# Attention and quantized convolution block: start, first block and seams reordered, with filler products on TensorE

## The chip, the core and the metric

The kernel runs on one core of a Trainium2 chip. The metric is the device time of one execution in microseconds (us); the median of three runs of the kernel before is 2590.27 us (2589.32 to 2590.64). The engines are TensorE (PE: products, with its weight loads PEld), VectorE (DVE), ScalarE (ACT), GpSimd (POOL) and SyncE (SP, which here only issues DMAs). Each works through its own queue in order and waits for the others by semaphores. Products are written to PSUM, which DVE and ACT read.

## What is computed

x has 4 images of 128 channels by 64 x 64 positions, all in float32. First attention with 4 heads of 32 channels over 4096 positions of an image, then a residual block of two 3x3 convolutions with quantized weights:

```python
x_norm = _group_norm(x, norm_w, norm_b)              # 8 groups of 16 channels
qkv = jnp.einsum('oc,bchw->bohw', qkv_w, x_norm) + qkv_b[None, :, None, None]
...
attn = jax.nn.softmax(jnp.einsum('bhid,bhjd->bhij', q, k) * scale, axis=-1)
out = jnp.einsum('bhij,bhjd->bhid', attn, v)
...
x = x + jnp.einsum('oc,bchw->bohw', proj_w, out) + proj_b[None, :, None, None]
...
out = conv3x3_decomposed(x, lsq_quantize(w1, alpha1))
out = jax.nn.relu(batchnorm(out, gamma1, beta1))     # mean and variance over all 4 images
out = conv3x3_decomposed(out, lsq_quantize(w2, alpha2))
out = jax.nn.relu(batchnorm(out, gamma2, beta2) + x)
```

Each batch norm needs the statistics of the whole convolution before its first output can be made. So there is a seam between the convolutions, and another before the final ReLU, at which the last statistics have to come through.

## The kernel before

**Stages.** Lines 564 to 585: image 0 is loaded in 8 chunks of 512 columns (tiles xh0 and xh1, four chunks each), its group statistics are made, and the first chunks of k, q and v. Lines 589 to 710: attention, in 32 blocks of 512 queries (4 images by 8), each with 32 steps kt of 128 keys. Lines 714 to 796: first convolution. Lines 798 to 837: second convolution. Lines 838 to 846: final sum, ReLU and store.

**A step of attention.** `scores` makes a half step: 4 products s (line 425, q and k each split into a high and a low part), and an exponential on ACT (427) into a tile p. `weights` adds p times v to acc (438), and p to a running sum on DVE (450); six of the 32 steps (MOVED) add theirs by a DMA of POOL instead (443, 445). PE's order is written out by hand: 3 half steps of scores, 1 step of weights, 3 half steps, 2 steps. Scores run ahead of weights. One such cycle of three steps has some 6.2 us of PE work, and more where side work is due.

**Side work.** `schedule` lists functions with the step kt after which they are emitted. In block n = 0 (lines 624 to 630) these are the remaining chunks of k, q and v of image 0: 16 or 32 products in two halves (301) into a bank of PSUM, then, one step later, the evacuation: for k and q the high part on ACT (335) and the low part on DVE (336), for v one addition on DVE (355). k and q go by a store on POOL's queue (340) to DRAM, and come back in another layout by SP's loads (394 for k, 405 for q). `load_q` of the next block is emitted at step 14. The first chunks, k_0 and q_0, go straight from the staging tile to their place (`direct`, lines 375 to 387), with 8 DMAs each, over SP and POOL in turns.

**PSUM and buffers.** Pool pss has 3 tiles of two banks (scores, the first chunks, later the convolution tiles), pool psa 2 tiles of one bank: acc holds one of them all through a block, and all side products take turns with the other. ppool has 8 tiles, for p and, at the start, for xh0, xh1 and the staging of the first chunks; a tile comes free when its last reader is done.

**Group statistics.** `norm_parts` returns steps that run alternately on DVE and PE: zero (aggregate the statistics of the chunks), one (average the means over a group by a product with gavg, gm), two (variance of the group's parts, dv), three (product gv), four (reciprocal root with POOL's power, scale ga, offset gc, scaled weights wn), five (products gb of the offsets with the weights, for the biases of k and q, and of v), six (add the biases). For image 0 they run in one go; for images 1 to 3 they are side work two blocks ahead.

**Convolutions.** The image is cut into 16 bands of 16 rows (4 images by 4); a band has two halves of 512 columns. `conv` makes 18 products for a half (9 taps by a high and a low part of the input, 722). `layer` runs the bands: both halves into one tile of two banks, `prepare` (splits or ReLUs of a coming band), then for each half statistics on DVE (774) and a copy to SBUF on ACT (775). At the end `batch_norm` aggregates the statistics of all 32 halves and makes scale and offset; in the second layer's input they are applied by `relu_rows`: ReLU on ACT into t (802), a rounding copy to hi (805) and the difference lo (806) on DVE.

Of the kernel before, what the change touches and what calls it, by code (L numbers as in the profile page):

```python
# [16 lines left out]
F32 = mybir.dt.float32  # L17
# [61 lines left out]
def _fast_body(ctx, tc, x, norm_w, norm_b, qkv_wt, qkv_b, proj_wt, proj_b,  # L79
# [31 lines left out]
    warm = const.tile([P, 1], F32, name="warm")  # L111
    nc.scalar.activation(warm, mhalf, AF.Exp)
# [124 lines left out]
    def norm_parts(b, st):  # L237
# [13 lines left out]
        def two():  # L251
            nc.vector.tensor_copy(mean, gm[0][:, 0:1])
            nc.vector.tensor_tensor(dv, mv[:, 0:1], mean, ALU.subtract)
            nc.vector.tensor_tensor(dv, dv, dv, ALU.mult)
            nc.vector.tensor_tensor(dv, dv, mv[:, 1:2], ALU.add)
# [5 lines left out]
        def four():  # L261
# [4 lines left out]
            nc.vector.tensor_tensor(c, mean, a, ALU.mult)  # L266
            nc.vector.tensor_tensor(c, nb, c, ALU.subtract)
# [7 lines left out]
        def five():  # L275
# [4 lines left out]
            nc.tensor.matmul(gm[2][:, P : 2 * P], cb, wqkv[:, 2 * P : 3 * P], start=True, stop=True)  # L280

        def six():
            b2 = wpool.tile([P, 2], F32, name=f"b2_{b}", tag="b2")
            nc.vector.tensor_tensor(b2, gm[2][:, 0:2], bkq, ALU.add)
            bvn = wpool.tile([P, P], F32, name=f"bvn{b}", tag="bvn")
            nc.vector.tensor_tensor(bvn, gm[2][:, P : 2 * P], bv, ALU.add)
            norm[b] = norm[b][0], b2, bvn

        return zero, one, two, three, four, five, six
# [4 lines left out]
    qs, ks, vs = {}, {}, {}  # L294

# [7 lines left out]
    def project_parts(b, j, xin, start=False):  # L303
# [5 lines left out]
        def bank(what):  # L309
            if start:  # L310
# [64 lines left out]
    def direct(what, t):  # L375

        u = k_tile(0, 0) if what == "k" else q_tile(0, 0)
        for g in range(2):
            for s in range(4):
# [3 lines left out]
                eng = (nc.sync, nc.gpsimd)[s % 2]  # L383
# [68 lines left out]
    def finish_parts(n):  # L452
# [30 lines left out]
        def sums_at_once():  # L483
# [6 lines left out]
            weigh()  # L490
            most = [small.tile([P, 1], F32, name=f"most{i}") for i in range(2)]
# [35 lines left out]
        return dict(copy=copy, merge=merge, sums=sums, sums_at_once=sums_at_once, spread=spread, invert=invert, gather=gather,  # L527
# [37 lines left out]
    for j in range(NB):  # L565
        eng = (nc.sync, nc.scalar)[j % 2]
        eng.dma_start(out=halves[j // 4][:, j % 4, :], in_=x_chunk(0, j))
    st = small.tile([P, NB, 6], F32, name="st0", tag="st")
    for j in range(NB):
        nc.vector.bn_stats(st[:, j, :], halves[j // 4][:, j % 4, :])  # L570
    for f in norm_parts(0, st):
        f()
# [8 lines left out]
    for what, j in (("k", 0), ("q", 0), ("k", 1), ("v", 0), ("k", 2), ("v", 1), ("k", 3), ("v", 2)):  # L581
        for f in first_chunk(j, what, True):
            f()
        if what == "v":
# [9 lines left out]
    def schedule(n, before):  # L594
# [27 lines left out]
        if n + 1 < len(blocks):  # L622
            add(14, lambda: load_q(*blocks[n + 1]))
# [682 lines left out]
```

## Time and profile before

The profiled execution took 2589.98 us; its span from the first to the last instruction is 2588.2 us. All times below are in us from the start of that span.

| what | where | time |
|---|---|---|
| x chunk 0, then chunk 1 reach DVE | start | 3.82, 8.48 |
| statistics of image 0 done | 570 | 13.02 |
| first products of k (pk) begin | 301 | 18.68 |
| first score product | 425 | 29.05 |
| first exponential, first acc product | 427, 438 | 30.45, 34.39 |
| last acc product of block 0 ends | 438 | 114.8 |
| first convolution product | 722 | 2265.87 |
| last product of the first layer ends | 722 | 2408.71 |
| first product of the second layer | 722 | 2415.49 |
| last product of the second layer ends | 722 | 2555.25 |
| first store of the output issued | 846 | 2562.62 |
| last store issued, end of the span | 846 | 2580.6, 2588.2 |

A busy share is an average over all these stages. What an edit is worth is read where it works: which engine waits there, for what, and whether something later waits for that engine.

### The profile page before, as it was taken

To read this page: it belongs to the slowest core of one execution; us is meant where nothing else is said; L and a number is where in the kernel's file an instruction comes from. 1 tells how busy PE (TensorE), PEld (TensorE's weight loads), DVE (VectorE), ACT (ScalarE), POOL (GpSimd) and SP (SyncE) were. 2 spreads that over 40 slices of the span, in tenths; PEclk is the share of its full clock that TensorE was granted. 3 is DMA by queue.
4 is the path that set the end of the run, shared out by engine and by line. 5 is a ranking of instruction groups with operands and counts; after the bars stand their busy time and mean duration, and the time that the engine had idled before them with its cause. 6 is when DMAs were issued, how large, how long until landed. Compare 5 with 4: busy or idle time off the path is not lost.

```text
span 2588.2 us, 48399 instructions
## 1 busy us (share of the span) xinstructions
PE 2517.2 (97%) x20394; PEld 1223.4 (47%) x20394; DVE 2140.3 (83%) x1402; ACT 2081.9 (80%) x2275; POOL 281.4 (11%) x456
## 2 busy tenths in 40 slices
PE   6999999999999999999999999999999999999894
PEld 3444444444444444444444444444444444477773
DVE  5898888888988898888988988888999998953344
ACT  4888899999988999999988899999889898911223
POOL 2111111111011111110011111110000000100000
PEclk9999999999999999999999999999999999999997
DMA  5876766698667767697667666986655757634004
GB/s 160 191 187 172 177 161 149 154 206 201 162 148 178 178 155 171 149 225 171 160 171 161 164 159 150 207 202 142 151 130 126 154 126 148 146 80 145 1 1 164
DMA packets 147417, 400.04 MB, mean 155 GB/s; under 512 B 59240, under 2 KB 60008, under 8 KB 118648
## 3 DMA queue, kind: packets, MB, share of 16 engines
q0 software_dynamic: 45888, 280.59, 47.9%
q1 hardware_dynamic: 100728, 115.23, 16.8%
q8 instruction: 162, 2.65, 0.4%
q10 hardware_dynamic: 576, 1.05, 0.1%
q14 instruction: 63, 0.52, 0.1%
HBM read 105.32 MB, written 55.83 MB: 62 GB/s over the span
## 4 chain that ended last, share of the span: by engine, by line
PE 88%; DVE 5%; issue 3%; DMA 2%; ACT 1%; POOL 0%; SPq 0%; DVEq 0%; POOLq 0%; ACTq 0%
PE s L425 39%; PE acc L438 34%; PE c L722 9%; DVE r L450 3%; DMA rm<-p 2%; PE l L467 1%; PE po L301 1%; PE pk L301 1%; PE pq L301 1%; PE pv L301 1%; ACT p L427 1%; DVE res L844 1%; DMA xh<-in_x_dram 0%; DMA q<-qst 0%; DVE st L570 0%
## 5 line engine op out<-in xcount | busy, mean ns | idle before, releaser
L427 ACT ACTIVATE p<-s 128x1024 f32<-128x1024 f32 x2048 | 1940.2, 1034 | 235.0 <-PE s L425 158.7
L450 DVE TENSOR_TENSOR r<-r,p 128x2048 f32<-128x2048 f32 x768 | 1758.4, 2290 | 97.3 <-ACT p L427 48.1
L425 PE MATMUL s<-q,k 64*128 64x512 f32 x8192 | 1162.3, 413 | 3.9 <-ACT p L427 2.2
L438 PE MATMUL acc<-p,v 128*32 128x512 f32 x8192 | 1021.1, 601 | 0.6 <-DVE v L355 0.6
L425 PEld LDWEIGHTS s<-q,k 64*128 64x128 f32 x8192 | 711.7, 185 | 631.9 <-issue 298.0
L438 PEld LDWEIGHTS acc<-p,v 128*32 128x32 f32 x8192 | 198.6, 109 | 453.7 <-issue 446.3
L445 POOL DMA_DIRECT2D rm<-p x160 | 138.6, 866 | 950.7 <-ACT p L427 783.6
L775 ACT COPY cv<-c 128x512 f32<-128x512 f32 x64 | 37.6, 587 | 220.8 <-DVE st L774 220.8
L722 PE MATMUL c<-hi,wq 128*128 128x512 f32 x576 | 150.1, 405 | 8.3 <-DVE hi L805 6.8
L722 PE MATMUL c<-lo,wq 128*128 128x512 f32 x576 | 148.1, 402 | 0.0
L774 DVE BATCH_NORM_STATS2 st<-c 128x6 f32<-128x512 f32 x64 | 44.7, 699 | 124.5 <-PE c L722 102.5
L722 PEld LDWEIGHTS c<-hi,wq 128*128 128x128 f32 x576 | 109.4, 191 | 40.1 <-issue 8.9
L722 PEld LDWEIGHTS c<-lo,wq 128*128 128x128 f32 x576 | 109.0, 189 | 28.9
L448 DVE TENSOR_TENSOR r<-p,p 128x2048 f32<-128x2048 f32 x32 | 73.3, 2291 | 25.0 <-ACT p L427 25.0
L336 DVE SCALAR_TENSOR_TENSOR kst<-pk,b,kst 128x512 fp32r<-128x512 f32 x32 | 24.0, 751 | 73.2 <-ACT kst L335 73.2
L336 DVE SCALAR_TENSOR_TENSOR qst<-pq,b,qst 128x512 fp32r<-128x512 f32 x32 | 24.0, 750 | 41.6 <-ACT qst L335 41.6
L471 POOL DMA_DIRECT2D r<-rm x31 | 26.3, 848 | 159.8 <-PE s L425 91.9
L340 POOL DMA_DIRECT2D qd<-qst x31 | 23.3, 753 | 177.6 <-DVE qst L336 130.2
L443 POOL DMA_DIRECT2D rm<-p x32 | 17.8, 556 | 223.3 <-ACT p L427 136.4
L335 ACT ACTIVATE kst<-pk,b 128x512 fp32r<-128x512 f32 x32 | 22.4, 701 | 21.7 <-PE pk L301 21.7
L340 POOL DMA_DIRECT2D kd<-kst x28 | 20.6, 734 | 167.6 <-DVE kst L336 159.6
L467 PE MATMUL l<-r,ones 128*32 128x256 f32 (+1 forms) x504 | 37.9, 383 | 0.5 <-issue 0.5
(129 smaller groups left out, 672.0 us busy)
## 6 DMA issues: line engine op xcount, KB each, us to landing
rm<-p POOLq DMA_DIRECT2D x192, 1024.0 KB, 7.9
q<-qd SPq DMA_DIRECT2D x248, 128.0 KB
r<-rm POOLq DMA_DIRECT2D x31, 1024.0 KB, 7.1
x<-in_x_dram SPq DMA_DIRECT2D x80, 256.0 KB
k<-kd SPq DMA_DIRECT2D x124, 128.0 KB
qd<-qst POOLq DMA_DIRECT2D x31, 512.0 KB, 6.9
kd<-kst POOLq DMA_DIRECT2D x28, 512.0 KB, 4.0
y<-x POOLq DMA_DIRECT2D x32, 256.0 KB, 5.0
```

Of the source, the lines that this page charges most:

```text
L301: nc.tensor.matmul(out[cs, :], w[:, cs], x, start=True, stop=True)
L336: nc.vector.scalar_tensor_tensor(lo, ps[what], bias, t[:, 0, :], ALU.add, ALU.subtract)
L340: (nc.sync if start else nc.gpsimd).dma_start(out=dst[b, j].rearrange("s p n -> p s n"), in_=t)
L425: nc.tensor.matmul(s[:, i, :], k[r, half, c0 : c0 + P], q[r, half, part, :], start=(part == 0), stop=(part == 1))
L427: nc.scalar.activation(pts[step][:, 2 * half : 2 * half + 2, :], s, AF.Exp, scale=SCALE)
L438: nc.tensor.matmul(acc[n][h * D : (h + 1) * D, :], v[:, kt % KB, h * D : (h + 1) * D], pt[:, h, :], start=(kt == 0), stop=(kt == NK - 1))
L445: nc.gpsimd.dma_start(out=msum[n], in_=pt, accum_op=ALU.add)
L448: nc.vector.tensor_tensor(rsum[n], pts[step - 1], pt, ALU.add)
L450: nc.vector.tensor_tensor(rsum[n], rsum[n], pt, ALU.add)
L467: nc.tensor.matmul(t["l"][h * D : (h + 1) * D, cs], ones, r[:, h, cs], start=first, stop=end)
L722: nc.tensor.matmul(ps[:, j, :].rearrange("p (r w) -> p r w", w=W), w[:, tap, :], part[:, j * RB + kh : j * RB + kh + RB, kw : kw + W], sta ...
L774: nc.vector.bn_stats(st[:, b * NB + c, :], ps[:, j, :])
```

## The change

Attention after block 0, and the convolutions between their ends, keep their instructions; these parts change:

- **Start.** ACT's activation that loads the function table moves behind ACT's four x loads. A new `keep_warm(count)` issues products of gavg with itself into a psa bank that nobody reads: 26 before the statistics of image 0, 3 behind gm, 6 behind gv, and 10 at the end of each convolution layer. In `norm_parts` some DVE operations are fused, mean is copied after dv, the signs of the offset are turned, and the product for v's bias with its addition become steps of their own (five_v, six_v), for image 0 after q_0. `direct` changes the order of its DMAs and takes ACT's queue in for q. v chunks at the start use psa; v_3 is made there.
- **First block.** The side chunks stand at least three steps apart; q_1 goes from step 2 to 18, and the load of q_1 from step 14 to 22.
- **First convolution's start.** `bounds` (maxima of the last block's sums) is split off and comes after the split of band 2.
- **Layers.** The two halves of the last band have a psa bank each, so that each has its own statistics; those of the other 30 halves are aggregated ahead, into columns 0 to 2 of `end`, as one set with its count, mean and squared deviation; `batch_norm` aggregates these 15 columns. Products with alpha are made beforehand.
- **Second layer's first band.** ReLU is done twice on ACT, once into hi and once into t; DVE only makes lo.
- **End.** The first piece of the output goes in two halves.

```diff
-    warm = const.tile([P, 1], F32, name="warm")
-    nc.scalar.activation(warm, mhalf, AF.Exp)
...
         def two():
+            nc.vector.tensor_tensor(dv, mv[:, 0:1], gm[0][:, 0:1], ALU.subtract)
+            nc.vector.scalar_tensor_tensor(dv, dv, dv, mv[:, 1:2], ALU.mult, ALU.add)
             nc.vector.tensor_copy(mean, gm[0][:, 0:1])
-            nc.vector.tensor_tensor(dv, mv[:, 0:1], mean, ALU.subtract)
-            nc.vector.tensor_tensor(dv, dv, dv, ALU.mult)
-            nc.vector.tensor_tensor(dv, dv, mv[:, 1:2], ALU.add)
...
-            nc.vector.tensor_tensor(c, mean, a, ALU.mult)
-            nc.vector.tensor_tensor(c, nb, c, ALU.subtract)
+            nc.vector.scalar_tensor_tensor(c, mean, a, nb, ALU.mult, ALU.subtract)
...
-            nc.tensor.matmul(gm[2][:, P : 2 * P], cb, wqkv[:, 2 * P : 3 * P], start=True, stop=True)
...
+        def five_v():
+            gm[3] = psa.tile([P, FB], F32, name=f"gw{b}", tag="a")
+            nc.tensor.matmul(gm[3][:, 0:P], norm[b][2], wqkv[:, 2 * P : 3 * P],
+                             start=True, stop=True)
...
+    def keep_warm(count):
+        t = psa.tile([P, FB], F32, name=f"idle{count}", tag="a")
+        for _ in range(count):
+            nc.tensor.matmul(t[:, 0:P], gavg, gavg, start=True, stop=True)
...
-            if start:
+            if start and what != "v":
...
+        engines = (nc.sync, nc.gpsimd) if what == "k" else (nc.scalar, nc.sync, nc.gpsimd)
         for g in range(2):
-            for s in range(4):
+            for c, s in enumerate((0, 2, 1, 3)):
...
-                eng = (nc.sync, nc.gpsimd)[s % 2]
+                eng = engines[(4 * g + c) % len(engines)]
...
+    table = const.tile([P, 1], F32, name="table")
+    nc.scalar.activation(table, mhalf, AF.Exp)
+    keep_warm(26)
...
+    zero()
+    one()
+    keep_warm(3)
+    two()
+    three()
+    keep_warm(6)
+    four()
+    five()
+    six()
...
-            add(14, lambda: load_q(*blocks[n + 1]))
+            add(22 if n == 0 else 14, lambda: load_q(*blocks[n + 1]))
         if n == 0:
-            for kt, what, j in ((0, "k", 4), (2, "q", 1), (3, "v", 3), (6, "k", 5), (9, "k", 6),
-                                (12, "v", 4), (15, "k", 7), (18, "v", 5), (21, "v", 6),
-                                (24, "v", 7)):
+            for kt, what, j in ((0, "k", 4), (3, "k", 5), (6, "v", 4), (9, "k", 6), (12, "v", 5),
+                                (15, "k", 7), (18, "q", 1), (21, "v", 6), (24, "v", 7)):
...
+                add(slots[0] + 1, late[b][7])
+                add(slots[0] + 2, late[b][8])
...
     split_band(*bandlist[2])
+    last["bounds"]()
...
-        nc.vector.bn_aggr(mv, st.rearrange("p j s -> p (j s)"))
-        v = small.tile([P, 1], F32, name=f"bv{i}", tag="dv")
-        nc.vector.tensor_scalar(v, mv[:, 1:2], alpha_s[i], alpha_s[i], ALU.mult, ALU.mult)
-        r = rsqrt_eps(v, f"br{i}")
+        nc.vector.bn_aggr(mv, st)
+        r = small.tile([P, 1], F32, name=f"br{i}", tag="rs")
+        nc.vector.tensor_scalar(r, mv[:, 1:2], a_q[i], EPS, ALU.mult, ALU.add)
+        nc.gpsimd.tensor_tensor(r, r, mhalf, ALU.pow)
+        na = small.tile([P, 1], F32, name=f"bn{i}", tag="dv")
+        nc.vector.tensor_tensor(na, r, a_n[i], ALU.mult)
+        c = small.tile([P, 1], F32, name=f"bc{i}", tag="gc")
+        nc.vector.scalar_tensor_tensor(c, mv[:, 0:1], na, bn[i][1], ALU.mult, ALU.add)
         a = small.tile([P, 1], F32, name=f"ba{i}", tag="ga")
-        nc.vector.tensor_scalar(a, r, alpha_s[i], bn[i][0], ALU.mult, ALU.mult)
-        c = small.tile([P, 1], F32, name=f"bc{i}", tag="gc")
-        nc.vector.tensor_tensor(c, mv[:, 0:1], a, ALU.mult)
-        nc.vector.tensor_tensor(c, bn[i][1], c, ALU.subtract)
+        nc.vector.tensor_tensor(a, r, a_g[i], ALU.mult)
...
+        nc.vector.bn_aggr(end[:, 1:3], st.rearrange("p j s -> p (j s)")[:, : 6 * B * NB - 12])
+        nc.vector.tensor_scalar(end[:, 2:3], end[:, 2:3], float((B * NB - 2) * FB), None, ALU.mult)
+        b, g = bandlist[-1]
+        for j in range(2):
+            ps = psa.tile([P, FB], F32, name=f"c{i}_last{j}", tag="a")
+            conv(ready[i, b, g], ps, j, wq[i])
+            c = 2 * g + j
+            nc.vector.bn_stats(end[:, 3 + 6 * j : 9 + 6 * j], ps)
+            nc.scalar.copy(cv[b][:, c * FB : (c + 1) * FB], ps)
+        prepare(len(bandlist) - 1)
+        keep_warm(10)
+        return batch_norm(i, end)
...
-    relu_band(*bandlist[0], pieces=((0, RB + 2), (RB + 2, BR + 2)))
+    for r0, r1 in ((0, RB + 2), (RB + 2, BR + 2)):
+        a, e = max(r0 + g0 * BR - 1, lo_row), min(r1 + g0 * BR - 1, hi_row)
+        for dst in (hi_inner.bitcast(F32R), t["inner"][0]):
+            nc.scalar.activation(dst[:, a - lo_row : e - lo_row, :],
+                                 cv[b0].rearrange("p (h w) -> p h w", w=W)[:, a:e, :], AF.Relu,
+                                 bias=c1, scale=a1)
+        nc.vector.tensor_tensor(t["lo"][:, r0:r1, :], f32(t["t"])[:, r0:r1, :],
+                                f32(t["hi"])[:, r0:r1, :], ALU.subtract)
...
-            y = res[b, j]
-            cs = slice(j * HN, (j + 1) * HN)
-            nc.vector.scalar_tensor_tensor(y, cv[b][:, cs], a2, y, ALU.mult, ALU.add)
-            nc.scalar.activation(y, y, AF.Relu, bias=c2)
-            nc.sync.dma_start(out=out[b].rearrange("c h w -> c (h w)")[:, cs], in_=y)
+            for p in range(2 if b == j == 0 else 1):
+                n = HN // 2 if b == j == 0 else HN
+                y = res[b, j][:, p * n : (p + 1) * n]
+                cs = slice(j * HN + p * n, j * HN + (p + 1) * n)
+                nc.vector.scalar_tensor_tensor(y, cv[b][:, cs], a2, y, ALU.mult, ALU.add)
+                nc.scalar.activation(y, y, AF.Relu, bias=c2)
+                nc.sync.dma_start(out=out[b].rearrange("c h w -> c (h w)")[:, cs], in_=y)
```

## Prediction

> **What bounds it.** I read the engine totals and the chain first, then the timeline where the change works: 0 to 36 us, the first block to 115, the seam of the convolutions at 2409, the end from 2555.
>
> ```profile
> PE 2517.2 (97%) x20394; PEld 1223.4 (47%) x20394; DVE 2140.3 (83%) x1402; ACT 2081.9 (80%) x2275; POOL 281.4 (11%) x456
> ...
> PE 88%; DVE 5%; issue 3%; DMA 2%; ACT 1%; POOL 0%; SPq 0%; DVEq 0%; POOLq 0%; ACTq 0%
> ```
>
> TensorE (PE) sets the time. Between 115 and 2409 us it has work almost throughout; what an edit there takes from another engine is worth nothing. What can be gained is where PE waits. Of the timeline, with start, duration, engine, line, out<-in and the wait before it:
>
> ```profile
> 13.05 0.37 DVE L244 BATCH_NORM_AGGREGATE mv<-st 128x2 f32<-128x48 f32 x1
> ...
> 18.68 1.94 PE L301 MATMUL pk<-xh,wn 128*32 128x256 f32 x16
> ...
> 20.69 0.69 ACT L335 ACTIVATE kst<-pk,b 128x512 fp32r<-128x512 f32 x1 [18.39 <-PE pk L301]
> ...
> 24.02 3.49 SPq L387 DMA_DIRECT2D q<-qst  x4
> ...
> 26.62 1.04 PE L301 MATMUL pk<-xh,wn 128*32 128x256 f32 x16
> ...
> 31.92 1.64 PE L425 MATMUL s<-q,k 64*128 64x512 f32 x11 [0.99 <-DMA q<-qst]
> ```
>
> Image 0 has its statistics at 13.02, its first k on ScalarE (ACT) at 20.69, and scores flow from 31.92, when the last of q_0 lands. The same 16 products take 1.94 at first and 1.04 later: PE begins at half clock (the granted clock reads 1.00 here, so the durations decide).
>
> ```profile
> 41.29 1.07 PE L301 MATMUL pq<-xh,wn 128*32 128x256 f32 x16 [1.52 <-DVE kst L336]
> ...
> 47.33 1.25 PE L301 MATMUL pv<-wn,xh 128*32 128x128 f32 x32 [2.38 <-DVE qst L336]
> ...
> 48.50 2.93 PE L425 MATMUL s<-q,k 64*128 64x512 f32 x12
> ...
> 87.58 1.07 PE L438 MATMUL acc<-p,v 128*32 128x512 f32 x8 [0.62 <-DVE v L355]
> ```
>
> In the first block, products of the side chunks stand 1.52 and 2.38 for a psa bank whose evacuation queues behind ACT's exponentials; then twelve score products take 2.93 instead of 1.66; at 87.58 acc waits for v_5, made two steps before its use.
>
> ```profile
> 2408.75 0.70 DVE L774 BATCH_NORM_STATS2 st<-c 128x6 f32<-128x512 f32 x1 [6.56 <-PE c L722]
> ...
> 2410.10 0.70 DVE L774 BATCH_NORM_STATS2 st<-c 128x6 f32<-128x512 f32 x1 [0.65 <-ACT cv L775]
> ...
> 2410.84 1.02 DVE L751 BATCH_NORM_AGGREGATE bmv<-st 128x2 f32<-128x192 f32 x1
> ...
> 2413.87 4.06 ACT L802 ACTIVATE t<-cv,bc,ba 128x576 f32<-128x576 f32 x4 [2.45 <-DVE bc L759]
> 2414.84 0.50 DVE L805 CAST hi<-t 128x660 fp32r<-128x660 f32 x1 [1.13 <-ACT t L802]
> ...
> 2415.49 4.18 PE L722 MATMUL c<-hi,wq 128*128 128x512 f32 x9 [6.77 <-DVE hi L805]
> ```
>
> At the seam PE's last product ends at 2408.71 and the next starts at 2415.49: 6.78. Statistics of the first half come only after both; the second waits for the copy of the first.
>
> ```profile
> 2564.00:2566.00 2.00, 0.00 (x0) 0.00 (x0) 2.00 (x2) 1.95 (x2) 0.00 (x0) 0.50 1.01 406
> ...
> 2582.00:2584.00 2.00, 0.00 (x0) 0.00 (x0) 0.00 (x0) 0.00 (x0) 0.00 (x0) 0.50 1.03 408
> ```
>
> Of the windows at the end (busy of PE, PEld, DVE, ACT, POOL, then granted clock, DMA share, GB/s): DMA is full (share 1.01 to 1.03, about 405 GB/s) from 2563.4 to 2584.3, whatever VectorE (DVE) and ACT do. The span's last 4 us stay.
>
> **Beginning.** Table load (1.28) and first activation now stand behind ACT's four x loads: those start at 0.81, not 1.91. DMA was already 0.87 to 0.95 full from 2 to 10 us, so x as a whole comes hardly earlier; but chunk 1 (ACT's) came at 8.48 while DVE had idled 3.97, and from there seven chunks cost DVE 4.54. Between 0 and -1.4 (DMA still ends at 10.2, with two statistics behind it); I take -1.0, so statistics end at S = 12.0. From there to k's evacuation took 7.67. Removed: two of four DVE operations ahead of gv (2 x 0.195 = 0.39; mean's copy goes behind), one ahead of gb (0.19), and the 128-wide product of cb (17.98 to 18.68: 0.70) with its wait. At full clock pk is 0.9 shorter and gm, gv, gb some 0.5 together. Sum 2.7: ACT starts k at S + 5.0 = 17.0, 3.7 earlier. The fused scalar operations have no row: 0.16 (two-tensor) to 0.28 (two pointers, L753); nearest 0.16 to 0.2.
>
> The idle products have no row either. Below: 0.22, the pitch of the one-column pair L279 once warm; above: 0.78, L280's busy time cold. L722 shows a 128-wide weight load hidden behind the product before it, so I take 0.5 cold, 0.27 warm. In the trace PE needed 4.9 of full work (18.68 to 23.6) to warm; 26 products then take 10 x 0.5 + 16 x 0.27, from 1.83 to 11.2, ahead of gm at 12.4. Three and six of them (0.8, 1.6) fill the waits of 0.83 and 1.55; overrun 0.1.
>
> q_0's eight loads go over SP, POOL and ACT. **A rule against it:** the Trainium skill's DMA: Bandwidth & Descriptors, Rules for kernel authors, says that spreading over issuing engines doesn't help bandwidth and saves only issue time. SP's four issues took 3.49, and DMA was 0.25, 0.56, 0.77 busy in 22 to 25, then near full to 31. By the rule nothing beyond -3.7; by the ramp about 1 more. I take -1.0: scores flow at 27.2, **-4.7** (ends -2 and -6.5). The price: ACT's three issues wait for DVE's low part of q, and kst_1, kst_2, kst_3 stand behind them, about 1.5 to 2 later; SP's store of kd_1 and the score banks wait for those. Cover: k_1 is needed at step 4, 7.9 after scores flow; it would arrive 2.5 before. v_3 (0.9 of PE) moves into the wait for q_0, its cover.
>
> **First block.** Side chunks stand three steps apart, as those from step 6 did without a wait. From the starts of score groups (36.25, 42.29, 48.50, 53.26; steady 3.44 per half cycle, visits 0.87 to 0.98 more), the excess is 1.6 + 2.75 + 1.3, and 0.8 at 84.3 to 88.6: 6.5. v_3 leaves: 0.98. Next in line is ACT, 6.4 busy of a 6.9 cycle. q_1 moves from step 2 to 18 with 16 products, two evacuations, POOL's store (past kd_5, kd_6, kd_7 and four moved p) and SP's eight loads (step 22, behind k_7's four): on the old axis landed at 95, needed at 101. Until step 18 q_1 keeps xh0, so p has a buffer less; p_9 takes p_4's, five steps on, where p_11 took it. Its POOL transfer (landing 6.9 to 11.1) would end at 49.3 to 54, p_9 is wanted at 51.5: 0 to 2.5, taken 0.5. **-7.0** (ends -3 and -8).
>
> Later images: the v-bias product moves one step on and waits for b2. In the trace DVE ran b2 at 197.66, 750.27, 1304.12, before PE was through that step (197.8, 751.2, 1305): nothing; if DVE lagged an add, 2.3 each.
>
> **First convolution.** The bounds (1.7) and six new scalars (1.1) come behind the split; the split stays behind the store, so PE's 1.56 before 2287.93 stays. Statistics start 2 later, band 3's high part at 2295, wanted at 2296.6: hidden, 1.6 to spare.
>
> **Seam.** After the last product at T: statistics of the second half 0.74, aggregate of 15 columns 0.25 (0.37 for 48, 1.02 for 192), r 0.2 to 0.3, POOL's power 0.70 with its waits, three scalars 0.6, ACT start 0.16, ReLU straight into hi 0.87, PE start 0.2: T + 3.85 instead of T + 6.78, -2.9. The aggregate of 30 halves (1.0) lies in DVE's wait of 6.5 ahead. lo needs a second ReLU and 0.84: T + 5.6, wanted T + 6.2. Ten products hold PE to T + 2.7. PE's first two groups took 6.53 instead of 4.30: -2.2. **The clock rule:** TensorE: Matmul & The Clock Gate, Part 1, lets it fall after an idle window of about 3.4. Here it fell 4.85 after the last product (0.76 granted in 2412 to 2415, 0.50 after), but also at 48.1 behind gaps of 1.52 and 2.38. By the rule a gap of 3.85 without products may already lose 2.2; by the second row even 2.4 can. With them the gap is 1.2 and neither loses it. **-5.1** (ends -2.9 and -5.5).
>
> **End.** The same chain saves 2.2; the first piece in halves issues its store at 3.98 after the last product instead of 7.37, but the next store comes at 6.4 (DVE 0.65, 0.65, 1.28, ACT 1.15), with 15 transfers of 1.29 behind it: 6.4 + 19.35 against 7.37 + 20.64. **-2.3** (ends -1.5 and -3.4). The ten products here hide nothing and cost nothing.
>
> **Sum:** -4.7 - 7.0 - 5.1 - 2.3 = -19.1. The profiled execution took 2589.98 (span 2588.2 and 1.8 around it), 0.3 under the median 2590.27; the same 19 off gives **2571**.
>
> **Rivals.**
> Block 0 keeps its stalls in another form (p_9's buffer, ACT 93% busy, late q_1): about 5 of 7 back, 2577. For: block 1 shows an exponential waiting 2.1 for a moved p. Against: the same spacing ran from step 6 without one. Chance 0.17.
> The products don't hold the clock (one-bank weights, small moving operand): start loses 1.5, seam 2.2: 2575. For: no row shows it; against: 128-wide products counted as work from 18.68 on. 0.10.
> The products block the queue: at a pitch of 0.86, two 0.43 halves without overlap and never warm, 26 end at 24.2 instead of before 12.4 (+11.8), three and six add 5.3, ten hold PE to T + 8.6 (+4.7), and the 2.2 of the cold seam come back. -19.1 + 11.8 + 5.3 + 4.7 + 2.2 = +4.9: 2595, slower. It decides from a pitch of about 0.75; L279 at 0.22 warm and L722's hidden loads speak against. 0.03.
> Statistics still wait for both halves, so that the change doesn't do what it says: 1.4 at seam and end each, 2574. Against: two tiles of one bank, written one after the other. 0.03.
>
> The forecast's own case (2566 to 2575) has 0.62, a larger gain 0.05. The range 2565 to 2580 takes in all but the queue and the tails. About 0.2%, 5 us, is what this measurement tells from no change: faster 0.95, same 0.03, slower 0.02.
>
> **What would show it.** First k on ACT near 17, scores flowing near 27; no PE wait over 1 between 36 and 55 on the old axis; the first block's last product about 11.7 earlier; next product 3.9 after the seam's last, at 2.3 per nine; the first store 4 after the last product. A gm that waits for idle products, an exponential waiting for a transfer, or a seam at half clock would make it wrong.

## The result, and the profile after

The changed kernel takes 2574.76 us (median of 6 runs, 2569.78 to 2577.97), the kernel before 2590.53 on the same chip: a ratio of 0.9935, 95% interval 0.9922 to 0.9948. The profiled execution took 2571.87, with a span of 2570.1; that is 18.1 less than the profiled execution of before. The medians differ by 15.8, since the runs of the changed kernel spread over 8 us and the profiled one is among the shorter.

Cut at the events that the prediction named, the two profiles give (ends of groups are start plus duration; the group in which block 0's acc products end also holds the first step of block 1, so that this mark, 114.87 before and 103.16 after, lies 0.86 behind the last product of block 0 itself, here and in every profile below):

| stretch | before | after | difference | forecast |
|---|---|---|---|---|
| start of the span to the flow of scores | 31.92 | 26.59 | -5.3 | -4.7 |
| from there to the last acc product of block 0 | 82.95 | 76.57 | -6.4 | -7.0 |
| from there to the first convolution product | 2151.00 | 2152.48 | +1.5 | 0 |
| from there to the first product of layer 2 | 149.62 | 146.52 | -3.1 | -2.9 |
| from there to the end of the span | 172.71 | 167.94 | -4.8 | -4.5 |

The first lines of the page of after, the engine totals and the shares of the chain of waits:

```profile
PE 2526.5 (98%) x20504; PEld 1231.7 (48%) x20504; DVE 2139.0 (83%) x1401; ACT 2083.9 (81%) x2278; POOL 280.3 (11%) x459
...
PE 82%; DVE 9%; DMA 4%; issue 3%; ACT 1%; POOL 0%; SPq 0%; DVEq 0%; POOLq 0%; ACTq 0%
```

PE is busier by 9.3 us although the kernel is shorter: the idle products count as work. In the chain of waits some of PE's share went to DVE and DMA, yet PE, busy for 98% of the span, is still the bound; the totals alone would mislead here. Timeline of after, the start (start, duration, engine, line, out<-in, count, wait before it; each idle product stands as two records, so that x52 are the 26):

```profile
1.89 8.95 PE L303 MATMUL idle<-gavg 128*128 128x128 f32 x52 [1.89 <-POOL mhalf L110]
...
11.53 0.37 DVE L242 BATCH_NORM_AGGREGATE mv<-st 128x2 f32<-128x48 f32 x1
11.96 0.38 PE L247 MATMUL gm<-mv,gavg 128*128 128x1 f32 x2 [1.12 <-DVE mv L242]
...
15.25 1.07 PE L310 MATMUL pk<-xh,wn 128*32 128x256 f32 x16
...
16.39 0.69 ACT L344 ACTIVATE kst<-pk,b 128x512 fp32r<-128x512 f32 x1 [12.19 <-PE pk L310]
...
17.25 0.69 ACT L344 ACTIVATE qst<-pq,b 128x512 fp32r<-128x512 f32 x1 [0.18 <-PE pq L310]
...
26.59 2.06 PE L435 MATMUL s<-q,k 64*128 64x512 f32 x12 [0.41 <-DMA q<-qst]
```

Statistics end at 11.5 (13.0 before), k is evacuated 4.9 later, as forecast, and k's 16 products take 1.07 at once: here PE is warm. The first block, same view:

```profile
38.27 1.67 PE L435 MATMUL s<-q,k 64*128 64x512 f32 x12
...
44.20 1.06 PE L310 MATMUL pv<-wn,xh 128*32 128x128 f32 x32
45.19 1.65 PE L435 MATMUL s<-q,k 64*128 64x512 f32 x12
...
85.36 1.06 PE L448 MATMUL acc<-p,v 128*32 128x512 f32 x8 [0.54 <-DVE v L364]
```

In this block no product waits for a bank any more, and from 31 to 91 us each twelve scores take 1.64 to 1.67. Only v_6's wait of 0.54 is left. The seam (x20 are the ten idle products):

```profile
2398.48 2.39 PE L303 MATMUL idle<-gavg 128*128 128x128 f32 x20
2398.68 0.70 DVE L825 BATCH_NORM_STATS2 end<-c_last 128x6 f32<-128x512 f32 x1 [3.59 <-PE c_last L752]
2399.41 0.22 DVE L790 BATCH_NORM_AGGREGATE bmv<-end 128x2 f32<-128x15 f32 x1
...
2401.15 0.87 ACT L877 ACTIVATE hi<-cv,bc,ba 128x576 fp32r<-128x576 f32 x1 [1.15 <-DVE ba L799]
...
2402.16 2.39 PE L752 MATMUL c<-hi,wq 128*128 128x512 f32 x9 [1.29 <-ACT hi L877]
```

From the last product of layer 1 to the first of layer 2 it is 3.5 us (6.78 before), of which PE stands 1.29, and the first nine products take 2.39 instead of 4.18. At the end, the store queue and one of the windows (busy of PE, PEld, DVE, ACT, POOL, then granted clock, DMA share, GB/s):

```profile
2543.81 10.99 SPq L914 DMA_DIRECT2D out_dram<-res  x10
```

```profile
2550.00:2555.00 5.00, 0.00 (x0) 0.00 (x0) 5.00 (x5) 4.81 (x5) 0.00 (x0) 0.50 1.01 402
```

The first store is issued 4.0 after the last product, and DMA is full again (share 1.01 in this window) while the output drains.

### The profile page after: what moved, and what is told of

It reads as the page before. It is cut to its first block, busy times and chain, and to the rows that moved or that the text cites. A ratio compares the mean times of both kernels' runs of the same rounds, so it can differ in the third digit from the quotient of the medians.

```text
span 2570.1 us, 48634 instructions
## 1 busy us (share of the span) xinstructions
PE 2526.5 (98%) x20504; PEld 1231.7 (48%) x20504; DVE 2139.0 (83%) x1401; ACT 2083.9 (81%) x2278; POOL 280.3 (11%) x459
## 3 DMA queue, kind: packets, MB, share of 16 engines
q10 hardware_dynamic: 720, 1.44, 0.2%
## 4 chain that ended last, share of the span: by engine, by line
PE 82%; DVE 9%; DMA 4%; issue 3%; ACT 1%; SPq 0%; POOL 0%; DVEq 0%; POOLq 0%; ACTq 0%
PE s L435 36%; PE acc L448 32%; PE c L752 9%; DVE r L460 6%; DMA rm<-p 4%; PE l L477 1%; PE pk L310 1%; PE pq L310 1%; PE po L310 1%; PE pv L310 1%; ACT p L437 1%; DVE res L912 1%; PE c_last L752 0%; DMA xh<-in_x_dram 0%; DVE r L458 0%
## 5 line engine op out<-in xcount | busy, mean ns | idle before, releaser
L752 PE MATMUL c<-hi,wq 128*128 128x512 f32 x540 | 139.2, 402 | 2.8 <-DVE hi L562 1.6
L752 PE MATMUL c<-lo,wq 128*128 128x512 f32 x540 | 138.6, 401 | 0.0
L752 PEld LDWEIGHTS c<-hi,wq 128*128 128x128 f32 x540 | 101.2, 188 | 32.5 <-DVE hi L562 2.5
L752 PEld LDWEIGHTS c<-lo,wq 128*128 128x128 f32 x540 | 101.6, 188 | 27.1
L310 PE MATMUL po<-av,wp 128*32 128x512 f32 x256 | 33.4, 594 | 4.2 <-DVE av L526 4.2
```

Of the source, the lines that this page charges most:

```text
L310: nc.tensor.matmul(out[cs, :], w[:, cs], x, start=True, stop=True)
L752: nc.tensor.matmul(ps.rearrange("p (r w) -> p r w", w=W), w[:, tap, :], part[:, r0 + kh : r0 + kh + RB, kw : kw + W], start=(n == 0), stop ...
```

## The experiments

Every variant below is the changed kernel with the edit that is shown. The time differences are between medians on the same chip; the changed kernel itself was 15.8 below the kernel before in its first runs and 17.9 in later ones, so a us or two between medians decides nothing by itself. What decides is the stretch in which the edit lies, read in the variant's own profile.

### The first block's order

```diff
-                    ("v", 3)):
...
-            add(22 if n == 0 else 14, lambda: load_q(*blocks[n + 1]))
+            add(14, lambda: load_q(*blocks[n + 1]))
...
+            for kt, what, j in ((0, "k", 4), (2, "q", 1), (3, "v", 3), (6, "k", 5), (9, "k", 6),
+                                (12, "v", 4), (15, "k", 7), (18, "v", 5), (21, "v", 6),
+                                (24, "v", 7)):
```

> The changed kernel with the first block's old order: v_3 back at step 3, q_1's products at step 2, its load at step 14, the side chunks one to three steps apart. Theory (the stalls of the first block come from this order alone): products wait 1.5 and 2.4 for a bank in the first 25 us of scores, twelve scores at half clock follow, and from the flow of scores to the last acc product it takes 82 to 83 us instead of 76.6, so the time is 6 to 7 us above the changed kernel's. Rival (the stalls came from the late beginning of the old kernel and would not come back with k and v earlier): 78 us or less, time at most 2 us above. On the scatter of the runs: if the new order is what makes it 8 us wide, here it is 3 us or less.

Median 2581.01, 11.8 below before, so 4.0 or 6.1 above the changed kernel, by which of its two figures is taken; 6 to 7 were expected. Its timeline, the waits of PE in the first block and the first scores:

```profile
27.97 4.43 PE L435 MATMUL s<-q,k 64*128 64x512 f32 x19 [1.97 <-DMA q<-qst]
...
39.35 1.07 PE L310 MATMUL pq<-xh,wn 128*32 128x256 f32 x16 [1.52 <-DVE kst L345]
...
45.40 1.15 PE L310 MATMUL pv<-wn,xh 128*32 128x128 f32 x32 [2.38 <-DVE qst L345]
```

The waits of 1.52 and 2.38 are back to the digit, though everything before them runs earlier: the order makes them, not the late beginning of the old kernel. Flow to last acc product takes 84.98, 8.4 more than in the changed kernel and 2 more than expected. Of these, some 1.8 are the 19 scores at half clock (4.43 against 19 x 0.138 = 2.6), because without v_3 PE stood 1.97 for q_0. The rest, 6.6, is the order with v_3's products. On the spread the expectation also held (2579.77 to 2581.91), but with four runs that is weak.

### The idle products at the start

```diff
-    keep_warm(26)
...
-    keep_warm(3)
...
-    keep_warm(6)
```

> The changed kernel without the 26, 3 and 6 idle products at its start; all else as changed. Theory (they bring TensorE to full clock before the first real product): gm, gv and gb take some 0.5 us more together and pk about 1.9 instead of 1.07, so ScalarE starts k_0 near 17.9 instead of 16.39, and scores flow near 28.2 instead of 26.59; from there nothing differs, so the time is 1.5 to 2 us above the changed kernel's. Rival (one-column products and k's product do not depend on them, or the wait for the mean's chain swallows it): scores flow within 0.3 of 26.6 and the time is the same. Second rival (without them TensorE is still cold when scores begin): first twelve scores at half clock, 3 us or more above.

Median 2576.56, 16.2 below before. Scores flow at 28.77 and block 0 ends at 105.83, against 26.59 and 103.16: against the first profile of the changed kernel the products are worth 2.2, then 2.7, a little more than expected. In the medians little of it is left, and the next runs show one reason.

The next run has no edit at all, it is the changed kernel once more:

> The changed kernel once more, unaltered, to see where its runs differ (they spread over 8 us, those of the kernel before over 4). Theory (in some runs the clock falls in a short gap of the start, before gm or before q_0 is there, and half clock then costs 1 to 2 us each): the excess of this profile over the first one's 2571.87 lies ahead of the last acc product of block 0 (103.16 in the first profile), with a granted clock near 0.5 for some 3 us between 12 and 36; from there to the end it is 2467 within 1.5. Rival (the attention blocks scatter, by exponentials that wait for moved p): block 0 ends at 103 to 104 in any case, and the stretch from there to the first convolution, 2152.5 in the first profile, takes the excess. Median 2573 to 2577.

Median 2573.81 (2572.43 to 2577.08). The profiled run was again one of the short ones (2572.49), so the excess that I wanted to place was not there to be seen: block 0 ended at 103.65, and the rest took 2467.2. This run settles nothing about the spread. Other variants that do not touch the start showed it. In the variant with band 2 split first (below), the windows of the start are:

```profile
10.00:12.00 2.00, 0.34 (x4) 0.15 (x2) 1.52 (x3) 0.00 (x0) 1.06 (x2) 1.00 0.05 9
12.00:14.00 2.00, 1.81 (x14) 1.81 (x15) 0.74 (x5) 0.00 (x0) 0.12 (x1) 0.93 0.02 1
14.00:16.00 2.00, 2.00 (x12) 2.00 (x11) 0.84 (x4) 0.00 (x0) 0.45 (x1) 0.50 0.00 0
```

PE worked 0.34 of the 2 us from 10 to 12, and the clock fell to 0.50 at 13.7, when PE had been busy again for 1.5 us. How long PE stood ahead of gm, and how long it took from gm to k's first product, in the nine profiles with 26 products at the start:

| wait ahead of gm | clock at 12 to 18 | gm to pk |
|---|---|---|
| 1.12, 1.44, 1.45 | 1.00 throughout | 3.29, 3.29, 3.30 |
| 1.61, 1.75, 1.85, 2.25 | down to 0.50 to 0.54 | 4.21, 4.49, 4.45, 4.62 |
| 2.94 (table load first), 3.31 | down to 0.50 to 0.51 | 4.63, 5.64 |
| no idle products | cold (pk takes 1.93) | 4.00 |

The wait differs mainly because the 26 products end anywhere from 9.3 to 10.9: each takes 0.43 until the clock rises and 0.22 after it, and in these nine profiles the clock rose anywhere from 4.77 to 8.00. When x lands adds the rest: the statistics' aggregate began at 11.40 to 12.20, with the table load first at 13.24. When the clock holds, the products win 0.7 on this piece; when it falls, they lose 0.2 to 1.6, since the three and six of them then take up to 1.6 and 2.9 at half clock in front of gv and gb. (k's own 16 products still gain: 1.93 without idle products, 1.07 to 1.53 with them.) So I let the last of them wait for x, as their right operand is x chunk 6:

```diff
-    keep_warm(26)
+    keep_warm(24)
+    keep_warm(7, halves[1][:, 2, 0:P])
```

> The changed kernel with 24 idle products at the start instead of 26, and 7 more that read the x chunk 6, so that they cannot start before it lands (some 10.2) and last until the mean is there (11.9). Theory (the clock falls in the gap of 1.1 to 2.3 between the last idle product and gm, in some runs): the gap ahead of gm is under 0.6, k's first products take 1.07 from 15.3 to 15.6 in the profile, ScalarE starts k_0 by 16.8, and the median is 1 to 3 us below that of the changed kernel run beside it, with a narrower spread. Rival (what scatters lies elsewhere): start as in the first profile, median and spread as of the kernel beside it. Second rival (seven products overrun): gm delayed by up to 0.6, the time 0.5 above.

Median 2571.64 (2569.99 to 2573.40), beside 2573.81 (2572.43 to 2577.08) of the changed kernel in the same runs. Its timeline:

```profile
10.80 1.83 PE L303 MATMUL idle<-xh,gavg 128*128 128x128 f32 x14 [1.02 <-DMA xh<-in_x_dram]
...
12.62 0.35 PE L247 MATMUL gm<-mv,gavg 128*128 128x1 f32 x2
```

In this profile and in the two later ones that have this edit gm follows the products without a wait, the clock stays at 1.00 from 10 to 20, and gm to pk is 3.26, 3.27, 3.26. PE now stands before the held products instead (1.02, 1.39 and 0.19), and the clock outlasted that. So the clock was held in three of three profiles, against three of nine without the edit. That the 2.2 in the medians is all from it is not shown: the ranges overlap, and block 0 ended at 104.35 here, no earlier than in the two profiles of the changed kernel (103.16, 103.65), since x came late (aggregate at 12.10).

### The queues of q_0, and the table load

```diff
-        engines = (nc.sync, nc.gpsimd) if what == "k" else (nc.scalar, nc.sync, nc.gpsimd)
+        engines = (nc.sync, nc.gpsimd)
```

> The changed kernel with q_0's eight loads on SP's and POOL's queues alone, in the new order, ScalarE's queue left out. Forecast's estimate (a third queue brings q_0 about 1 us earlier): scores flow at 27.6 instead of 26.59, time 1 us above. The rule of DMA: Bandwidth & Descriptors (more issuing engines save only issue time): the issues on SP become four of about 0.9, so the last is issued at most 0.9 later, and DMA, which is near full, lands all at 26.6 to 27; time the same within 0.5. Third: ScalarE gets to kst_1 to kst_3 near 18.9 instead of 20.79, so v's products no longer wait in this stretch, and the time is the same or up to 0.5 below.

Median 2576.18, 16.6 below before. From k's evacuation to the flow of scores it takes 9.89 without ACT's queue and 10.20 with it (9.8 to 10.8 in the other profiles that have it): the rule was right, a third issuing engine brought the last of q_0 no earlier. Yet block 0 ended 2.0 later than in the first profile, at 105.16, of which 0.36 is that ACT began k at 16.75 instead of 16.39:

```profile
26.64 1.76 PE L435 MATMUL s<-q,k 64*128 64x512 f32 x6 [2.46 <-DMA q<-qst]
```

In the changed kernel four score products ran at 25.18, as soon as the first parts of q_0 were there, and the wait left was 0.41. Here none could, PE stood 2.46, and the clock was granted at 0.53 to 0.62 from 28 to 32. Two things made this one wait longer: the first parts of q_0 came later, and v's products no longer waited, as the third expectation had it, so that PE was through with them at 24.18 instead of 25.25. The length of the wait also varies with the third queue in place (up to 1.3 where v_3 is made at the start), so that 2.0 is one draw and not the worth of the queue.

```diff
+    table = const.tile([P, 1], F32, name="table")
+    nc.scalar.activation(table, mhalf, AF.Exp)
     for j in range(NB):
...
-    table = const.tile([P, 1], F32, name="table")
-    nc.scalar.activation(table, mhalf, AF.Exp)
...
-            for p in range(2 if b == j == 0 else 1):
-                n = HN // 2 if b == j == 0 else HN
+            for p in range(1):
+                n = HN
```

> The changed kernel with two of its parts undone at two far places, each read in its own stretch: ScalarE's table load ahead of its four x loads again, and the first piece of the output whole. Start, theory (ScalarE's chunks decide when VectorE can go on): the statistics end 1.0 to 1.5 later (12.5 to 13.0 instead of 11.50), the gap between the 26 idle products and gm grows beyond 2 and the clock is lost, so that scores flow 2 us later or more. Rival (DMA is near full, so x lands at the same time whoever issues first): statistics end at 11.5 to 11.9. End, forecast's sum: the first store comes 5.2 instead of 3.96 behind the last product, but 16 transfers of 1.29 stand behind it instead of 15 behind 6.4, so the end comes 30.2 behind the last product as before, no change. Rival (the half piece's transfer is gained): 0.6 to 1.2 later.

Median 2577.55, 13.7 below before. Start: the aggregate begins at 13.24 instead of 11.53, 1.7 later. In the twelve profiles with the table load behind the x loads it begins at 11.40 to 12.20, in the two with it ahead at 13.05 (the kernel before) and 13.24, so the place of the table load is worth 0.9 to 1.8 there:

```profile
13.24 0.37 DVE L242 BATCH_NORM_AGGREGATE mv<-st 128x2 f32<-128x48 f32 x1
...
13.66 0.38 PE L247 MATMUL gm<-mv,gavg 128*128 128x1 f32 x2 [2.94 <-DVE mv L242]
```

PE then stood 2.94, the clock fell, and scores flow at 29.39, 2.8 later. End: from the last product (the start of the idle products behind it) to the end of the span 30.45, against 30.41 with the first piece in halves: the halves are worth nothing that shows, as the forecast's sum had it.

### The seam

```diff
-        keep_warm(10)
```

> The changed kernel without the ten idle products at the end of each convolution. Theory (they hold the clock): the gap at the seam stays 3.5 us, but the first two groups of nine products behind it take 6.5 us together instead of about 4.6, so the second convolution is about 2 us longer and the kernel too. Rival (a gap of 3.5 is short enough: in the kernel before the clock fell 4.85 after the last product): the first groups take 2.3 each, the time is unchanged, and the products hide nothing. In both cases the end of the kernel is unchanged.

Median 2575.25, 17.5 below before. The restart, and the windows around it:

```profile
2402.68 3.85 PE L752 MATMUL c<-hi,wq 128*128 128x512 f32 x9 [3.47 <-POOL t L550]
```

```profile
2402.00:2404.00 2.00, 1.32 (x4) 1.11 (x5) 0.55 (x1) 2.00 (x4) 0.00 (x0) 0.77 0.00 0
2404.00:2406.00 2.00, 2.00 (x6) 1.51 (x6) 1.00 (x2) 2.00 (x4) 0.24 (x3) 0.50 0.00 0
2406.00:2408.00 2.00, 2.00 (x9) 1.60 (x8) 1.87 (x2) 1.24 (x1) 0.00 (x0) 0.88 0.00 0
```

A gap of 3.47 lost the clock, and from the restart to the end of the span it takes 169.42 instead of 167.94: the products are worth 1.5 there, not 2. (The wait is put down to a POOL memset; the ReLU of ACT into hi came after it.)

```diff
-            ps = psa.tile([P, FB], F32, name=f"c{i}_last{j}", tag="a")
-            conv(ready[i, b, g], ps, j, wq[i])
+        ps = conv_tile(i, b, g)
+        for j in range(2):
+            conv(ready[i, b, g], ps[:, j, :], j, wq[i])
+        prepare(len(bandlist) - 1)
+        for j in range(2):
```

> The changed kernel with the last band of each layer in one tile of two banks again, so that the statistics of its first half wait for both halves (aggregate of 15 columns, double ReLU and idle products kept). Theory (each part of the seam's chain is worth what it takes on VectorE): the second half's statistics end 1.35 later (0.65 wait for the copy and 0.70), so the gap at the seam is 4.9 instead of 3.5, and the first store comes 5.3 instead of 3.96 after the last product; together 2.7 us above, and 1.5 more if the clock falls in the longer gap behind the idle products. Rival (the copy does not hold the second statistics): gap 4.2 at most, 1.4 in all.

Median 2576.75, 14.9 below before. The first convolution's stretch grew by 1.30, PE stood 2.59 behind the idle products, the first nine products took 3.64 instead of 2.39, and restart to end grew by 2.60, of which 1.3 are the same delay at the output:

```profile
2403.36 3.64 PE L752 MATMUL c<-hi,wq 128*128 128x512 f32 x9 [2.59 <-POOL t L550]
```

Sum 3.9, within the theory's 2.7 to 4.2: single banks are worth 1.3 at each layer's end, and 1.3 more where the longer wait loses the clock.

```diff
-        for dst in (hi_inner.bitcast(F32R), t["inner"][0]):
-            nc.scalar.activation(dst[:, a - lo_row : e - lo_row, :], ...
+    relu_band(*bandlist[0], pieces=((0, RB + 2), (RB + 2, BR + 2)))
```

> The changed kernel with the first band of the second layer made as before: ReLU into t on ScalarE, then a rounding copy into hi on VectorE, for both row pieces; the idle products stay. Theory (one more hop of 0.5 with its semaphore, and a clock that is lost once TensorE stands for more than about 1.5: in the profiles so far waits of 1.02, 1.12, 1.29, 1.44 and 1.45 at the start and the seam kept it, 1.61, 1.75, 1.85, 1.97, 2.25, 2.46 and 2.59 lost it): the wait behind the idle products grows from 1.29 to 1.9, and the first nine products take 3.4 to 3.9 instead of 2.39; 0.6 and 1.3 together, the time 1.9 above. Rival (the hop alone): 0.6, the first nine still at 2.4. Second rival (the lower part of the band comes earlier now and a later wait goes): less than 0.6.

Median 2575.63, 15.7 below before. The start of this profile was a bad one (the idle products ended at 9.31, the earliest of all, the aggregate began at 12.20, and PE stood 3.31), which has nothing to do with the edit. At the seam:

```profile
2408.09 2.42 PE L752 MATMUL c<-hi,wq 128*128 128x512 f32 x9 [1.87 <-DVE hi L858]
```

The stretch up to the restart is 0.56 longer and the clock held. So the hop through DVE costs 0.6, the plain rival, and my threshold of 1.5 fell: 1.87 kept the clock here. The last section shows why no single length will do.

### Towards a better version

```diff
+    split_band(*bandlist[2])
     last["project"]()
     last["store"]()
-    split_band(*bandlist[2])
```

> The changed kernel with the split of band 2 emitted ahead of the last block's projection and store. Theory (TensorE waits 1.56 near 2277.7 because VectorE splits band 2 only behind the store, and its data is there 5 us before): that wait goes, no other takes its place, and the stretch from the first to the last product of the first convolution is 1.5 shorter (143.0 to 141.5), the time 1.5 below the changed kernel's. Rival (the data or a buffer of band 2 comes just before): the wait stays, 0. Second rival (the projection now waits): a new wait ahead of it, up to 1 us, and the rest of the gain is lost.

Median 2573.14. The wait of 1.56 for band 2 is gone and no other came; from the first convolution product to the restart it takes 144.87 instead of 146.52. This profile lost the clock at the start (shown above), and its median is only 0.7 below that of the changed kernel beside it.

```diff
-            add(slots[9] - 2, before["weigh"])
+            add(slots[9] - 4, before["weigh"])
```

> A version meant to beat both: the changed kernel with the idle products held to gm by x chunk 6 (2.2 us lower in the median before), band 2 split ahead of the last store (1.6 lower in its stretch), and av times rc two steps earlier in every block (TensorE waits 4.2 us for it in image 3: 0.41, 2.45 and 1.35 near 1839, 1911 and 2047). Theory (these are three separate waits of TensorE): the waits for av go, block 0 to first convolution takes 2147 to 2149 instead of 2152.5, first convolution 141.2, median 8 us below the changed kernel's 2573.8, so about 2566, and 0.990 of the kernel before. Rival (VectorE is late as a whole in image 3, so the wait only moves to another reader, of r's additions or of the exponentials' buffers): half or none of the 4.2 is had, 2568 to 2570.

Products held to gm and band 2 split first are in it as shown above.

Median 2568.51 (2568.31 to 2573.17), 22.8 below before: ratio 0.9917, 0.9903 to 0.9930. The waits for av went, but at one of the three places the timeline shows what took their place:

```profile
1912.82 1.04 PE L310 MATMUL po<-av,wp 128*32 128x512 f32 x8
...
1921.04 1.06 PE L448 MATMUL acc<-p,v 128*32 128x512 f32 x8 [2.13 <-DVE x L536]
```

The projection now runs early, its bank waits for a late DVE, and acc of the next block needs the bank: the rival. PE's waits for av or for that bank are 2.8 in all instead of 4.2. The attention stretch was 2151.07, inside the range of 2150.85 to 2153.81 that the variants without this edit show (2150.34 in the next version, which also has the edit): a gain is not shown. PE also stood 1.24 for q_0, and the clock was 0.50 from 29 to 32.

```diff
+    keep_warm(4)
+
     late, xin = {}, {}
```

> The combined version with four more idle products, 0.96 us at full clock, between v_3 and the first scores. In its profile before, TensorE stood 1.24 for q_0 at 25.9 to 27.2, and the granted clock was 0.50 from 29 to 32. Theory (that wait loses the clock in some runs, at some 1.5 us each): the wait for q_0 is under 0.5, the clock is 1.00 from 14 to 36, scores flow at 27.2 or earlier for the same landing of q_0, and the last acc product of block 0 ends at 103 to 104.3; the median is 0.3 to 1.0 below the combined version's (2568.51), and the spread under 4. Rival (where q_0 is there early, the four products only push the scores back): scores 0.3 to 0.6 later, median equal or 0.5 above. The stretch from block 0 to the first convolution is not touched and may differ by 3, so the start alone decides between them.

Median 2568.99 (2567.57 to 2571.82), 22.9 below before, ratio 0.9917 (0.9903 to 0.9930). In the profile the wait for q_0 and the loss of clock are gone, scores flow at 26.83, and block 0 ends at 104.03. The median is no lower than without the four products, so neither theory is shown by it. Both versions are shorter than the kernel before beyond doubt, and their medians lie below each of the eleven runs of the changed kernel (the shortest 2569.78); their intervals of the ratio still overlap those of the changed kernel.

## Why the prediction was right, point by point

The sum of -19.1 was borne out by the two profiles (-18.1), stretch by stretch; in the medians it is -15.8, so 2574.76 stands 3.8 above the forecast of 2571. One term came out by luck, and one cost was put at nothing.

- **Statistics at S = 12.0.** They ended at 11.5, and at 11.4 to 12.2 in the other profiles. The term "-1.0" for the x loads was somewhat small: the place of the table load is worth 0.9 to 1.8. The first chunk came later than before (5.09 instead of 3.82), but from then on VectorE waited 1.18 for chunks instead of 4.15.
- **S + 5.0 to k on ACT.** Right where the clock holds: 4.9, with warm products and the shorter chain; 6.6 without idle products. The warm-up itself was taken as a fixed 4.9 of work. The clock rose 5.5 after pk began in the kernel before (at 24.21), and 2.9 to 6.1 after the first idle product in the later profiles.
- **q_0 about 1 earlier by a third queue.** Wrong, and the size was luck. The rule that was set against it held; without ACT's queue the same stretch is no longer (9.89 against 10.20). The stretch still shrank by 1.0, from 11.23. A term that I left out may explain up to 0.84 of it: q's 16 products are warm too, so ACT starts q 0.86 behind k (16.39 to 17.25) instead of 1.70 (20.69 to 22.39). No run sets it apart: without idle products, where q is 1.71 behind again, the stretch is 10.62, between the two.
- **First block -7.0.** Right in mechanism, as undoing it shows, and 0.6 too large. The 0.5 for p_9's buffer, set against it, was not seen at all, so the 6.5 of stalls was oversized by 1.1.
- **Nothing in the rest of attention.** +1.5 in this pair of profiles. In the ten later profiles without the edit of av the same stretch, with the same code, took 2150.85 to 2153.81; the 2151.00 of before lies in that range. No cost of the change is shown there. What makes this stretch differ by 3 us stays open; PE's waits for an exponential (0.7 us in the shortest, 3.1 in one of the longest) and the number of falls of the clock in it (none to two) go with it only loosely. The v-bias product, also put at nothing, waits 0.3 for b2 here and 1.0 in three of the variants.
- **Seam -2.9 and -2.2.** Right: -3.1 in the stretch (the gap alone went from 6.78 to 3.5), and in restart to end -2.1 beside the end's share. Single banks give 1.3 of the gap and the direct ReLU 0.6; the aggregate, 0.22 instead of 1.02, gives 0.8 by the timeline. The products are worth 1.5 once the gap is short.
- **End -2.3.** -2.7, all from the same chain; the halves give nothing, as worked out.
- **The rival that the products don't hold the clock (0.10)** came true in part: in six of nine profiles they did not hold it at the start. My sum had them end at 11.2, 1.2 ahead of gm at 12.4, and put that wait at nothing; they ended 1.1 to 3.3 before it. That, and a wait for q_0, is what the profile of a single good run could not show, and it fits the 3 us by which the median stands above the profiled run. That the clock held three times of three with the products held to gm supports it; the unprofiled runs can't be looked into, so the rest of the spread is not explained.

## What to carry to other kernels

Filler products are only as good as the wait that they leave: tie the last of them to data that comes just ahead of what the next real product waits for, and know that in a chain of short dependent steps they stand in its way once the clock is lost. Where a wait on the critical engine is removed, look at whether its buffer's next user takes the wait over, as the bank of the projection did. When a kernel's runs spread more than before, one profile is a draw: compare the stretches of several.

## What the runs showed of the hardware

The clock was lost far sooner than I had thought, and not by a fixed length of wait. It was lost behind waits of 1.24 and 1.28 (for q_0), 1.61 and more, and kept behind 1.44 and 1.45 (gm), 1.56 (band 2), 1.87 (seam) and even 2.46 to 2.48 (for av). It fell some 2 to 5 us after the wait had begun, mostly when PE was busy again.

What counts is where the wait lies in time. In all fourteen profiles every change of the granted clock, up or down, lies on one grid with a pitch of 3.41 us, to within 0.01 us over the whole span, and only the place of the grid differs from profile to profile. In that of the changed kernel the changes are at 7.95, 1912.59, 1916.00 and 2544.05: 558, 1 and 184 steps of 3.4133. A fall comes at the end of a step in which PE has stood. One wait tests this twelve times, since it is almost the same in twelve profiles (2.44 to 2.52, in image 3, for av) and only the grid cuts it differently. In the changed kernel it is

```profile
1911.05 1.07 PE L310 MATMUL po<-av,wp 128*32 128x512 f32 x8 [2.45 <-DVE av L526]
```

| the most that PE stood in one step there | profiles | clock behind it |
|---|---|---|
| 1.40, 1.69, 1.77 | 3 | 1.00 throughout |
| 1.87 to 2.52 | 9 | 0.50 for the next step |

Counted over all profiles, from the first rise to the end of the second convolution, each of the 21 steps in which PE stood 1.8 or more lost the clock. Of those with 1.24 to 1.77, five lost it and most did not; what decides among these stays open. A lost clock stayed at 0.50 for one step of 3.41 in most cases, and for two steps at two places, which cost 1.2 to 1.8 us where it could be set apart. The rises lie on the same grid, which is why the idle products at the start take more or less time from one execution to the next.

The Trainium skill, TensorE: Matmul & The Clock Gate, Part 1, describes a window of about 3.4 us that runs freely, and these traces agree with it (3.41). That the clock falls only after such a window of idleness they do not bear out: 1.8 us of a step was always enough. The advice of the same page, under Why this matters for your kernels, to avoid gaps over about 3 us is too generous for these runs, which lost the clock behind 1.24.
